# A graph layer's edge sums: 72 directly summed columns instead of 48, with three bf16 addends in place of fp32 operands

## The chip, the cores and the metric

The kernel runs on one NeuronCore of a Trainium2 chip. The metric is the device time of one execution in microseconds (us), lower is better. All times, spans and durations below come from that core.

## The reference

`x` has 6250 nodes with 128 features, there are 206250 edges, each with 128 fp32 features, and `src` names the node of each edge. What is computed, cut to what matters:

```python
edge_aggr = zeros((6250, 128)).at[src].add(edge_attr)            # sum of each node's edges
combined  = concatenate([x, edge_aggr, global_expand], -1) @ W_c + b_c
h = softplus(combined @ W1 + b1)
h = softplus(h @ W2 + b2)
x = layernorm(x + h @ W3 + b3)
```

Nearly all of the time goes into the first line: the edges are in no order of `src`, so each of the 206250 rows has to find its node.

## The kernel before

**Columns and groups.** The edges are laid out as 128 partitions by 1612 columns (the last is partial); a column is 128 edges. Columns 0 to 47 are summed directly. The other 1564 go through ten groups (`GROUPS`: 40, 120, 200, 240, 240, 240, 212, 140, 88 and 44 columns, called groups 0 to 9 here). For a group, DVE and PE work out a position for each edge (`positions`), so that edges of the same block of 256 nodes stand together in DRAM. POOL then writes each column to its positions with one indirect DMA (`scatter_rows`, L644). When the whole group is written, it is read back in chunks of 1024 rows (`reduce_steps`): DVE makes a one-hot matrix `hot` of 8 tiles of 128 rows against 256 nodes (L423), PE multiplies (L437: 8 tiles of 128x256, each recorded as two fp32 matmuls, so "x16"), and DVE adds the product onto `sums_t` (L454). While group g is scattered, group g-1 is reduced.

**The direct sum.** `direct_steps` takes columns in sets of 12 (`SET`). For each set and each of 13 windows of 512 nodes, ACT makes a one-hot of two columns: two `Abs` of 128x512 (L577) and one `Relu` of 128x1024 (L579), into `direct_hot`, of which there are four buffers. PE multiplies the columns' rows with it (L589: two fp32 matmuls of 512, recorded as four), adding up in the PSUM tile `direct_sum` (two buffers). After the set's 12 columns DVE adds that tile onto `sums_t` (L593). Two columns in one window are one *job* here: 24 x 13 = 312 jobs. The multiplication of a job stands two jobs behind its comparison.

**The order of the work.** PE, DVE, ACT and SP follow an order written out by hand: whatever stands first in an engine's queue holds up what is behind it. The main loop goes through *pieces* of 10 columns. For piece i it issues, in this order: the loading of the rows of piece i+3 (SP's queue), a copy of the node codes next to the rows of piece i+2 (ACT, L636), the ten scatters of piece i (POOL), and then a share of everything else: the next group's positions, the reduction of the group before, in groups 3 to 5 also the transposes and products of the nodes' own features, and a share of the direct steps. A scatter needs its piece's copy L636, and that copy stands in ACT's queue behind all direct comparisons of the steps before it.

The direct steps are spread over groups 1 to 6 in proportion to `left`:

```python
left[g] = max(0.0, groups[g][1] - groups[g][0]
              - groups[g - 1][3] * groups[g - 1][2] / 3 - (9 if 3 <= g < 6 else 0))
...
direct_at += len(direct) * left[g] / sum(left) / len(mine)
```

that is: the group's columns, less a third of the tiles of the reduction that runs in it, less 9 where the nodes' work is placed. There are 64, 168, 296, 336, 336, 336, 308, 188, 136 and 68 tiles in groups 0 to 9. So groups 1 to 6 have shares of 98.7, 144.0, 132.3, 119.0, 119.0 and 100.0.

After group 9's reduction, three small layers and the layer norm finish the nodes.

Of the kernel before, what the change touches and what calls it, by code (L numbers as in the profile page):

```python
# [7 lines left out]
F32 = mybir.dt.float32  # L8
BF16 = mybir.dt.bfloat16
# [3 lines left out]
ALU = mybir.AluOpType  # L13
# [3 lines left out]
P = 128  # L17
# [2 lines left out]
LOAD_COLS = 10  # L20
EPS = 1e-5

GROUPS = ((40, 1), (120, 2), (200, 4), (240, 4), (240, 4), (240, 4), (212, 4), (140, 2), (88, 2),
          (44, 1))
CHUNK_ROWS = 1024
PLACES = 3

DIRECT = 48
SET = 12
WIDE = 512  # L30
QUAD = 2
FILL = 4
POS_COLS = 20
PART_COLS = 60
# [13 lines left out]
def kernel(  # L48
# [23 lines left out]
    nc = tc.nc  # L72
    N, D = x.shape
# [8 lines left out]

    ND = min(DIRECT, T) // QUAD * QUAD
    c0 = ND
# [83 lines left out]
    with ExitStack() as phase:  # L168
        keep = phase.enter_context(tc.tile_pool(name="keep", bufs=1))
# [4 lines left out]
        direct_p = phase.enter_context(tc.tile_pool(name="direct", bufs=1))  # L174
# [17 lines left out]
        def whole_nodes(c0, c1):  # L192
            n = c1 - c0
            part = src_i[:, c0:c1]
            node = per.tile([P, C_MAX], F32, name="node", bufs=1)[:, :n]
            wrap = per.tile([P, C_MAX], F32, name="wrap", bufs=1)[:, :n]
            nc.vector.tensor_copy(node, part)
            nc.vector.tensor_scalar(wrap, node, 0.0, float(N), op0=ALU.is_lt, op1=ALU.mult)
            nc.vector.tensor_add(node, node, wrap)
            nc.vector.tensor_scalar(node, node, -1.0, float(N), op0=ALU.max, op1=ALU.min)  # L200
            nc.vector.tensor_scalar(wrap, node, 0.0, float(N + 1), op0=ALU.is_lt, op1=ALU.mult)
            nc.vector.tensor_add(part, node, wrap)
            return part, node, wrap
# [341 lines left out]
        def direct_steps():  # L545


            steps = []
            if not ND:
                return steps  # L550
            NW = -(-NB * BL // WIDE)
            less = keep.tile([P, NW, ND], F32, name="less")
            rows_in, hot_of, sum_of = {}, {}, {}

            def begin():

                first = keep.tile([P, NW], F32, name="first")
                nc.gpsimd.iota(first, pattern=[[WIDE, NW]], base=0, channel_multiplier=0,
                               allow_small_or_imprecise_dtypes=True)
                part, node, _ = whole_nodes(0, ND)  # L560
                nc.vector.tensor_copy(node, part)
                nc.vector.tensor_tensor(
                    less, node.unsqueeze(1).to_broadcast([P, NW, ND]),
                    first.unsqueeze(2).to_broadcast([P, NW, ND]), op=ALU.subtract)

            def load(c):
                n = min(SET, ND - c)
                rows_in[c] = direct_p.tile([P, SET, D], F32, name="direct_rows", bufs=2)
                sync_dma(rows_in[c][:, :n],
                         edge_attr[:P * T, :].rearrange("(p t) d -> p t d", p=P)[:, c:c + n, :])  # L570

            def compare(c, w, q):
                n = min(WIDE, NB * BL - w * WIDE)
                hot = direct_p.tile([P, QUAD, WIDE], F32, name="direct_hot", bufs=4)
                hot_of[c, w, q] = hot
                for j in range(QUAD):
                    nc.scalar.activation(hot[:, j, :n], iota_f[:, :n], AF.Abs,  # L577
                                         bias=less[:, w, c + q + j:c + q + j + 1], scale=-1.0)
                nc.scalar.activation(hot[:, :, :n], hot[:, :, :n], AF.Relu, bias=ones[:, :1],  # L579
                                     scale=-1.0)  # L580

            def add(c, w, q):
                n = min(WIDE, NB * BL - w * WIDE)
                k = min(SET, ND - c)
                hot = hot_of.pop((c, w, q))
                if q == 0:
                    sum_of[c, w] = ps.tile([P, WIDE], F32, name="direct_sum", bufs=2)
                for j in range(QUAD):
                    nc.tensor.matmul(sum_of[c, w][:, :n], rows_in[c][:, q + j, :], hot[:, j, :n],  # L589
                                     start=(q + j == 0), stop=(q + j == k - 1))  # L590
                if q + QUAD == k:
                    here = sums_t[:, w * WIDE:w * WIDE + n]
                    nc.vector.tensor_add(here, here, sum_of.pop((c, w))[:, :n])  # L593

            jobs = [(c, w, q) for c in range(0, ND, SET) for w in range(NW)
                    for q in range(0, min(SET, ND - c), QUAD)]
            steps += [begin, lambda: load(0)]
            for i in range(len(jobs) + 2):
                def one(i=i):
                    if i < len(jobs):  # L600
                        c, w, q = jobs[i]
                        if (w, q) == (NW // 2, 0) and c + SET < ND:
                            load(c + SET)
                        compare(*jobs[i])
                    if i > 1:
                        add(*jobs[i - 2])
                steps.append(one)
            return steps
# [10 lines left out]
        def load_rows(i):  # L619
            if i >= len(pieces):  # L620
                return
            g, c, k, r = pieces[i]
            rows = rows_p.tile([P, LOAD_COLS, W], F32, name="rows")
            rows_at[i] = rows
            if r == P:
                rows_dma(
                    rows[:, :k, :D],
                    edge_attr[:P * T, :].rearrange("(p t) d -> p t d", p=P)[:, c:c + k, :])
            else:
                rows_dma(rows[:r, 0, :D], edge_attr[P * T:, :])  # L630
# [21 lines left out]
        with tc.manual_schedule(engines={ET.PE, ET.DVE, ET.Activation, ET.SP}):  # L652
            nc.scalar.add_instruction(mybir.InstLoadActFuncSet(
                name=nc.get_next_instruction_name(), act_func_set_id=TABLES))
# [32 lines left out]
            direct = direct_steps()  # L687
# [3 lines left out]
            for g in range(1, G - 3):  # L691
                left[g] = max(0.0, groups[g][1] - groups[g][0]
                              - groups[g - 1][3] * groups[g - 1][2] / 3 - (9 if 3 <= g < 6 else 0))
            direct_at = 0.0
            i = 0
            assert G > 6
            nodes = []
            for g in range(G):
                mine = [q for q in range(len(pieces)) if pieces[q][0] == g]
                prep = []  # L700
                if g + 1 < G:
                    prep = [lambda g=g: node_codes(*groups[g + 1][:2])] + positions(g + 1)
                sums = reduce_steps(g - 1) if g else []

                if g == 3:
                    nodes = node_rows()
                other = nodes[:-(-len(nodes) // (6 - g))] if 3 <= g < 6 else []
                if 3 <= g < 6:
                    nodes = nodes[len(other):]
                filled = fill_rows(g + 1)  # L710
                done = [0, 0, 0, 0]
                for q in mine:
                    load_rows(i + LEAD)
                    code_rows(i + LEAD - 1)
                    scatter_rows(i)
                    i += 1

                    now = []
                    for w, todo in enumerate((prep, sums, other, filled)):
                        share = (q - mine[0] + 1) / len(mine)  # L720
                        if w == 2:
                            share = (share - 0.8) / 0.15
                        else:
                            share = share / AHEAD[w]
                        share = max(0.0, min(1.0, share))
                        upto = int(round(len(todo) * share))
                        now.append(todo[done[w]:upto])
                        done[w] = upto
                    if left[g]:
                        k = int(direct_at + 0.5)  # L730
                        direct_at += len(direct) * left[g] / sum(left) / len(mine)
                        now.append(direct[k:int(direct_at + 0.5)])

                    for _, _, step in sorted(
                            (((k + 0.5) / len(part), w, step) for w, part in enumerate(now)
                             for k, step in enumerate(part)), key=lambda t: t[:2]):
                        step()
# [111 lines left out]
    with tc.manual_schedule(engines={ET.PE, ET.DVE, ET.Activation, ET.SP}):  # L849
# [3 lines left out]
        for step in range(len(order) + 2):  # L853

            first, second, third = (order[k] if 0 <= k < len(order) else None
                                    for k in (step, step - 1, step - 2))
# [9 lines left out]
            if third:  # L866
                k = part_of[third]
# [29 lines left out]
```

## Time and profile before

| what | value |
|---|---|
| median of three runs | 2163.2 us (2162.69 to 2173.22) |
| the profiled execution's own time | 2166.67 us |
| its span, first to last instruction | 2164.9 us |
| mean granted TensorE clock | 0.925 |
| PE busy | 1789.7 us (83%) |
| POOL busy | 1560.2 us (72%) |
| DVE busy | 1328.0 us (61%) |
| ACT busy | 912.7 us (42%) |
| POOL, indirect DMAs (L644), 1564 of them | 1503.2 us |
| PE, reduction (L437) | 1106.0 us |
| PE, direct sum (L589) | 559.0 us |
| DVE, one-hots of the reduction (L423) | 592.2 us |
| ACT, direct comparisons (L577, L579) | 404.6 and 348.0 us |

A group's line on the profile's page names the source line, the engine, the operation and the tiles (out<-in), then the count, the busy time, the mean duration of one in ns, and behind the second bar the idle time of the engine just before such instructions and what ended most of it. In the timeline a line has its start and its length in us, and in brackets the idle time of the engine before it and what released it. The scatters run from 25.6 to 2019.3 us.

### The profile page before, as it was taken

What the parts mean: (1) busy time and instruction counts of PE and PEld (TensorE: products, weight loads), DVE (VectorE), ACT (ScalarE), POOL (GpSimd) and SP (SyncE); (2) the same over time, 40 slices, a digit from 0 to 9 for tenths busy, and PEclk for the clock granted to TensorE, in tenths of its full rate; (3) what the DMA queues carried; (4) which work ended last, traced back from release to release, by engine and by line L of the source; (5) the groups of instructions that cost most, each with busy time, mean ns of one, the idle gap of its engine ahead of it and who ended that gap; (6) DMA issues with size and microseconds to landing.
All of it is one profiled execution on the core that took longest, in us unless ns stands there. A gap on an engine that the chain in (4) does not pass through costs nothing.

```text
span 2164.9 us, 22230 instructions
## 1 busy us (share of the span) xinstructions
PE 1789.7 (83%) x6415; PEld 1209.0 (56%) x6415; DVE 1328.0 (61%) x1923; ACT 912.7 (42%) x1350; POOL 1560.2 (72%) x1631
## 2 busy tenths in 40 slices
PE   3398788966889878999889998788998899688884
PEld 0144445534555555666556666556666778566752
DVE  7386457524656345675465855355755798796567
ACT  0476665653444335444353443353342000006964
POOL 5777777777777767777777777777777777777226
PEclk8699999987999999999999999999999999899997
DMA  9998788738786665676756666556766687776521
GB/s 299 303 313 270 216 256 251 231 101 262 213 225 189 194 193 148 188 207 188 198 173 180 194 190 175 169 167 189 202 198 170 211 245 227 214 213 199 151 75 60
DMA packets 415376, 435.50 MB, mean 201 GB/s; under 512 B 37743, under 2 KB 305766, under 8 KB 415254
## 3 DMA queue, kind: packets, MB, share of 16 engines
q1 hardware_dynamic: 365062, 330.71, 54.9%
q0 software_dynamic: 50048, 103.35, 14.4%
q8 instruction: 51, 0.84, 0.2%
q14 instruction: 71, 0.58, 0.1%
q10 hardware_dynamic: 144, 0.02, 0.0%
HBM read 260.90 MB, written 173.03 MB: 200 GB/s over the span
## 4 chain that ended last, share of the span: by engine, by line
PE 57%; DVE 15%; POOL 9%; issue 7%; DMA 6%; ACT 4%; DVEq 1%; SPq 0%; POOLq 0%; ACTq 0%
PE part L437 37%; PE direct_sum L589 16%; POOL place L644 8%; DVE hot L423 7%; DMA place<-rows,pos 4%; DVE sums_t L454 2%; ACT hot L418 2%; DVE so_far L316 1%; DVE sums_t L593 1%; DMA rows<-in_edge_attr 1%; DMA chunks<-place 1%; PE small L339 1%; POOL y L833 1%; DVEq L448 1%; DVE pos L350 1%
## 5 line engine op out<-in xcount | busy, mean ns | idle before, releaser
L644 POOL DMA_INDIRECT place<-rows,pos x1564 | 1503.2, 961 | 509.0 <-issue 443.5
L437 PE MATMUL part<-hot,chunks 128*128 128x256 f32 x4472 | 1106.0, 405 | 267.8 <-DVE hot L423 250.9
L437 PEld LDWEIGHTS part<-hot,chunks 128*128 128x128 f32 x4472 | 894.9, 203 | 507.8 <-DVE hot L423 310.5
L577 ACT ACTIVATE direct_hot<-iota_f,less 128x512 f32<-128x512 f32 (+1 forms) x624 | 404.6, 695 | 811.0 <-PE direct_sum L589 808.1
L423 DVE SCALAR_TENSOR_TENSOR hot<-chunks,iota_ps 128x2048 f32<-128x2048 f32 (+1 forms) x261 | 592.2, 2270 | 44.2 <-DMA chunks<-place 44.2
L589 PE MATMUL direct_sum<-direct_hot,direct_rows 128*128 128x512 f32 (+1 forms) x1248 | 559.0, 580 | 29.4 <-DMA direct_rows<-in_edge_attr 25.6
L454 DVE TENSOR_TENSOR sums_t<-sums_t,part 128x256 f32 x781 | 327.1, 419 | 133.3 <-PE part L437 110.8
L589 PEld LDWEIGHTS direct_sum<-direct_hot,direct_rows 128*128 128x128 f32 x1248 | 233.3, 190 | 232.2 <-issue 204.9
L579 ACT ACTIVATE direct_hot<-direct_hot,ones 128x1024 f32<-128x1024 f32 (+1 forms) x312 | 348.0, 1115 | 10.1
L593 DVE TENSOR_TENSOR sums_t<-sums_t,direct_sum 128x512 f32<-128x512 f32 (+1 forms) x52 | 34.7, 667 | 410.5 <-PE direct_sum L589 410.5
L636 ACT COPY rows<-src_i 128x10 f32<-128x10 f32 (+1 forms) x159 | 30.7, 196 | 360.3 <-DMA place<-rows,pos 328.9
L350 DVE TENSOR_REDUCE pos<-at 128x20 int32<-128x500 f32 (+2 forms) x80 | 87.0, 1087 | 2.7
L316 DVE TENSOR_TENSOR_SCAN so_far<-iota_ps,ib 128x1500 bf16<-128x1500 f32 (+5 forms) x29 | 85.7, 2955 | 0.0
L418 ACT ACTIVATE hot<-iota_f,chunks 128x256 f32<-128x256 f32 x156 | 64.2, 493 | 26.7 <-DMA chunks<-place 24.2
L845 POOL TENSOR_TENSOR x_sb<-x_sb,b_all 128x512 f32<-128x512 f32 (+1 forms) x13 | 15.2, 1219 | 67.8 <-DMA x_sb<-in_x 67.8
L348 DVE TENSOR_TENSOR at<-small,ib 128x500 f32<-128x500 f32 (+2 forms) x80 | 52.9, 661 | 4.2 <-PE small L339 3.5
L833 POOL TENSOR_SCALAR y<-y,mv,rs 128x128 f32<-128x128 f32 (+1 forms) x45 | 35.2, 796 | 19.9 <-DVE rs L827 19.0
L262 DVE TENSOR_TENSOR ib<-block,iota_ps 128x1500 bf16<-128x1500 bf16 (+5 forms) x29 | 44.2, 1550 | 0.0
L273 PE MATMUL small<-ib,ones_h 128*128 128x500 bf16 (+2 forms) x80 | 23.8, 406 | 23.9 <-DVE ib L262 23.9
L536 DVE TENSOR_SCALAR z_x<-small,z_bias 128x512 f32<-128x512 f32 (+1 forms) x13 | 9.3, 718 | 51.3 <-PE small L534 51.3
L335 PE MATMUL small<-so_far,ones_h 128*128 128x500 bf16 (+2 forms) x80 | 31.4, 393 | 11.1 <-DVE last L319 11.1
L420 ACT ACTIVATE hot<-hot,ones 128x2048 f32<-128x2048 f32 (+1 forms) x20 | 39.2, 1960 | 0.7
(115 smaller groups left out, 472.7 us busy)
## 6 DMA issues: line engine op xcount, KB each, us to landing
chunks<-place SPq DMA_DIRECT2D x278, 516.0 KB, 4.5
rows<-in_edge_attr SPq DMA_DIRECT2D x155, 640.0 KB, 6.7
place<-fill SPq DMA_DIRECT2D x252, 258.0 KB, 8.3
place<-rows,pos POOLq DMA_INDIRECT x1564, 4.5
x_sb<-in_x SPq DMA_DIRECT2D x24, 256.0 KB, 4.6
direct_rows<-in_edge_attr SPq DMA_DIRECT2D x4, 768.0 KB
out<-y SPq DMA_DIRECT2D x12, 256.0 KB, 2.2
chunks<-place SPq DMA_DIRECT2D x3, 258.0 KB, 3.2
```

Of the source, the lines that this page charges most:

```text
L316: nc.vector.tensor_tensor_scan(t, iota_ps[:, 1:2].to_broadcast([P, NB * n]), in_block[k][0], 0.0, op0=ALU.mult, op1=ALU.add)
L350: nc.vector.tensor_reduce(pos[:, a - c0 + j0:a - c0 + j1], at.rearrange("p b g -> p g b"), axis=mybir.AxisListType.X, op=ALU.add)
L418: nc.scalar.activation(hot[:, j], codes, AF.Abs, bias=chunks[i][:, j, D:W], scale=-1.0)
L423: nc.vector.scalar_tensor_tensor(hot[:, :m], chunks[i][:, :m, D:W].to_broadcast([P, m, BL]), code_of(g), iota_ps.unsqueeze(1).to_broadcast ...
L437: nc.tensor.matmul(part[:, s - q, :], t[:, s * sub + j, :D], hot[:, s * sub + j], start=(j == 0), stop=(j == sub - 1))
L454: nc.vector.tensor_add(here, here, part[:, s - q, :])
L577: nc.scalar.activation(hot[:, j, :n], iota_f[:, :n], AF.Abs, bias=less[:, w, c + q + j:c + q + j + 1], scale=-1.0)
L579: nc.scalar.activation(hot[:, :, :n], hot[:, :, :n], AF.Relu, bias=ones[:, :1], scale=-1.0)
L589: nc.tensor.matmul(sum_of[c, w][:, :n], rows_in[c][:, q + j, :], hot[:, j, :n], start=(q + j == 0), stop=(q + j == k - 1))
L593: nc.vector.tensor_add(here, here, sum_of.pop((c, w))[:, :n])
L644: s = nc.gpsimd.indirect_dma_start(out=dst, out_offset=bass.IndirectOffsetOnAxis(ap=at, axis=0), in_=rows[:r, j, :], in_offset=None)
L833: engine.tensor_scalar(y[:r, q, :], y[:r, q, :], mv[:r, at + q, 0:1], rs[:r, 1, at + q:at + q + 1], op0=ALU.subtract, op1=ALU.mult)
```

## The change

`DIRECT` goes from 48 to 72, and group 6 from 212 to 188 columns, so that 24 columns are summed directly instead of being scattered and reduced. The fp32 operands of the direct matmuls become bf16. Each fp32 number x is written as three bf16 numbers whose sum is x: the upper half of its bits, the upper half of what is then left, and the rest. DVE does this in `split`, two columns at a time with three instructions; the first two addends are put into the two halves of the fp32 row itself, the third into a new tile `direct_low`. The one-hots, which hold ones and zeros, become bf16 tiles. A job now has six bf16 matmuls instead of two fp32 ones. There are 36 x 13 = 468 jobs, and 6 sets x 13 = 78 additions of `direct_sum` instead of 52. The window offsets `less` are computed for each set instead of once. The load of the first set moves ahead, to group 0's last piece. Group 6's reduction has 284 tiles instead of 308. The core of the diff:

```diff
-GROUPS = ((40, 1), (120, 2), (200, 4), (240, 4), (240, 4), (240, 4), (212, 4), (140, 2), (88, 2),
+GROUPS = ((40, 1), (120, 2), (200, 4), (240, 4), (240, 4), (240, 4), (188, 4), (140, 2), (88, 2),
...
-DIRECT = 48
+DIRECT = 72
...
+SPLIT = 2
...
+            def halves(t):
+
+                return [t.bitcast(BF16).rearrange("p c (d h) -> p c d h", h=2)[:, :, :, h]
+                        for h in (0, 1)]
+
+            def split(c):
+
+                n = min(SET, ND - c)
+                less = less_of[c] = direct_p.tile([P, NW, SET], F32, name="less", bufs=2)
+                nc.vector.tensor_tensor(
+                    less[:, :, :n], node_f[:, c:c + n].unsqueeze(1).to_broadcast([P, NW, n]),
+                    first.unsqueeze(2).to_broadcast([P, NW, n]), op=ALU.subtract)
+                low_in[c] = direct_p.tile([P, SET, D], BF16, name="direct_low", bufs=2)
+                for a in range(0, min(SET, ND - c), SPLIT):
+                    b = min(a + SPLIT, SET, ND - c)
+                    rest = direct_p.tile([P, SPLIT, D], F32, name="direct_rest")[:, :b - a]
+                    x_c = rows_in[c][:, a:b]
+                    nc.vector.tensor_sub(rest, x_c, halves(x_c)[1])
+                    nc.vector.tensor_sub(low_in[c][:, a:b], rest, halves(rest)[1])
+
+                    nc.vector.tensor_copy(halves(x_c)[0], halves(rest)[1])
...
-                hot = direct_p.tile([P, QUAD, WIDE], F32, name="direct_hot", bufs=4)
+                hot = direct_p.tile([P, QUAD, WIDE], BF16, name="direct_hot", bufs=4)
...
-                for j in range(QUAD):
-                    nc.tensor.matmul(sum_of[c, w][:, :n], rows_in[c][:, q + j, :], hot[:, j, :n],
-                                     start=(q + j == 0), stop=(q + j == k - 1))
+                for j in range(q, q + QUAD):
+                    addends = halves(rows_in[c][:, j:j + 1]) + [low_in[c][:, j:j + 1]]
+                    for i, part in enumerate(addends):
+                        nc.tensor.matmul(sum_of[c, w][:, :n], part[:, 0], hot[:, j - q, :n],
+                                         start=(j == 0 and i == 0), stop=(j == k - 1 and i == 2))
...
-            steps += [begin, lambda: load(0)]
+
+            steps += [lambda: load(0), begin, lambda: split(0)]
...
+                        if (w, q) == (NW - 2, 0) and c + SET < ND:
+                            split(c + SET)
...
+            direct_first = direct[:1]
+            direct = direct[1:]
...
+                    if g == 0 and q == mine[-1]:
+                        for step in direct_first:
+                            step()
```

More of the change, by code (lines that the diff above doesn't have):

```diff
@@ L551, in direct_steps @@
             NW = -(-NB * BL // WIDE)
-            less = keep.tile([P, NW, ND], F32, name="less")
-            rows_in, hot_of, sum_of = {}, {}, {}
+            node_f = keep.tile([P, ND], F32, name="node_f")
+            first = keep.tile([P, NW], F32, name="first")
+            less_of = {}
+            rows_in, low_in, hot_of, sum_of = {}, {}, {}, {}
             def begin():
-                first = keep.tile([P, NW], F32, name="first")
                 nc.gpsimd.iota(first, pattern=[[WIDE, NW]], base=0, channel_multiplier=0,
                                allow_small_or_imprecise_dtypes=True)
[L560 to L564, printed above, removed]
+                part, _, _ = whole_nodes(0, ND)
+                nc.vector.tensor_copy(node_f, part)
             def load(c):
@@ L577, in compare @@
                     nc.scalar.activation(hot[:, j, :n], iota_f[:, :n], AF.Abs,
-                                         bias=less[:, w, c + q + j:c + q + j + 1], scale=-1.0)
+                                         bias=less_of[c][:, w, q + j:q + j + 1], scale=-1.0)
                 nc.scalar.activation(hot[:, :, :n], hot[:, :, :n], AF.Relu, bias=ones[:, :1],
```

## Prediction

> **What bounds the kernel now.** I read first the page's groups, then POOL's waits, the timeline at the longest of them, and last a table of stages. The page:
>
> ```profile
> L644 POOL DMA_INDIRECT place<-rows,pos x1564 | 1503.2, 961 | 509.0 <-issue 443.5
> ```
>
> A scatter takes 0.96 us, and 0.30 pass before the next: 1.265 us a column, 12.65 a piece of ten. 1564 x 1.265 = 1978 of the 1994 us between the first scatter and the last; nearly nothing holds POOL up. Taken alone this says that 24 columns fewer save 24 x 1.265 = **30.4 us**. But a second chain runs level with POOL. POOL's longest wait behind the copy L636 is 9.3 us:
>
> ```profile
> 811.05 0.19 ACT L636 COPY rows<-src_i 128x10 f32<-128x10 f32 x1
> ...
> 811.52 0.96 POOL L644 DMA_INDIRECT place<-rows,pos  x1 [9.28 <-ACT rows L636]
> ```
>
> The copy came late, because it stands in ACT's queue behind direct comparisons, which wait for PE to free `direct_hot`. So I compared, over the run, when the copy for the third piece of a group was made (ACT's first work in that group) and when that piece was scattered: group 3 465.3 and 511.6, group 4 816.0 and 824.2, group 5 1123.5 and 1127.9, group 6 1432.2 and 1432.7 (POOL waits 1.46 us), group 7 1686.2 and 1700.9. In groups 1 and 2 the lead is above 36 us, as far as the row buffers allow; group 3 eats it up, and from there to group 6 ACT's copies come just in time. The stages between these copies (us; PE, PEld, DVE, ACT and POOL busy; clock; DMA share; GB/s):
>
> ```profile
> 465.00:816.00 351.00, 274.61 (x921) 181.96 (x921) 167.20 (x196) 140.02 (x200) 259.79 (x271) 0.87 0.71 205
> 816.00:1123.50 307.50, 273.32 (x976) 183.58 (x975) 188.33 (x227) 132.66 (x184) 233.48 (x244) 0.96 0.66 190
> 1123.50:1432.20 308.70, 270.08 (x968) 184.75 (x967) 180.41 (x216) 127.64 (x185) 233.69 (x244) 0.95 0.63 179
> 1432.20:1686.20 254.00, 229.10 (x864) 163.26 (x863) 155.49 (x176) 100.86 (x150) 192.62 (x201) 0.97 0.64 183
> ```
>
> PE is busy for 87 to 90% of the last three. The rest is the wait for one-hots, 96.0 us in 42 pieces from 816 to 1686. One of them:
>
> ```profile
> 913.35 1.88 PE L589 MATMUL direct_sum<-direct_hot,direct_rows 128*128 128x512 f32 x4
> ...
> 915.07 0.38 PE L334 MATMUL small<-ib,upto_h 128*128 128x500 bf16 x1
> ...
> 915.26 0.69 DVE L593 TENSOR_TENSOR sums_t<-sums_t,direct_sum 128x512 f32<-128x512 f32 x1 [9.07 <-PE direct_sum L589]
> ...
> 915.28 0.37 PE L335 MATMUL small<-so_far,ones_h 128*128 128x500 bf16 x1
> ...
> 915.49 0.37 PE L336 MATMUL small<-more,ones_h 128*128 128x500 bf16 x1
> ...
> 915.87 2.28 DVE L423 SCALAR_TENSOR_TENSOR hot<-chunks,iota_ps 128x2048 f32<-128x2048 f32 x1
> ...
> 918.21 4.97 PE L437 MATMUL part<-hot,chunks 128*128 128x256 f32 x14 [2.03 <-DVE hot L423]
> ```
>
> DVE waits 9 us in its queue for the job that ends a window, adds it (L593), and only then makes the next one-hot; PE stands idle for it. PE, with these waits, is the bound of groups 3 to 6 beside POOL. So the question is whether the change makes that chain longer.
>
> **The change part by part.**
>
> *Scatters.* 24 fewer, -30.4 us, only where POOL paces. From group 7 on, after the last direct step, it does: the rest then follows the scatters, so the end moves as group 7's third piece does.
>
> *A job on PE.* Before, four records: 913.35 to 915.07, 1.72 us. After, six bf16 matmuls of 512. The nearest rows are L334 to L336 above: starts 0.21 apart with 500 columns, weight loads hidden; six make 1.29. Three quarters of the cost, one and a half times the jobs. The addends' loads read every second bf16; bf16 loads took 0.10 and fp32 ones 0.19, both hidden in the rows, and 0.19 would still fit under 0.21, so I cost them at nothing.
>
> On that price the Trainium skill disagrees with itself: "TensorE: Matmul & The Clock Gate", section "Back-to-back issue gap", gives about 131 ns for a sustained 512-column matmul with its load, and 216 isolated. By 131 a job would be 0.79, and POOL would pace to the end. The 0.21 of the rows here is against it.
>
> *Jobs per group.* The direct steps go from 316 to 472 (the load left out), and the shares of `left` fall only in group 6, to 76.0, of 689 in sum. Groups 1 to 6 get 67.6, 98.6, 90.7, 81.5, 81.5, 52.1 steps after, against 43.7, 63.8, 58.6, 52.7, 52.7, 44.3. PE's change: group 3 90.7 x 1.29 - 58.6 x 1.72 = +16.2; groups 4 and 5 105.1 - 90.6 = +14.5 each; group 6 67.2 - 76.2 = -9.0. The reductions in groups 3 to 6 stay: the 24 tiles saved are group 6's, multiplied in group 7, where PE isn't the bound.
>
> *A job on ACT.* Each comparison is queued ahead of the copies:
>
> ```profile
> 462.89 1.32 ACT L577 ACTIVATE direct_hot<-iota_f,less 128x512 f32<-128x512 f32 x2
> 464.24 1.15 ACT L579 ACTIVATE direct_hot<-direct_hot,ones 128x1024 f32<-128x1024 f32 x1
> 465.29 0.19 ACT L636 COPY rows<-src_i 128x10 f32<-128x10 f32 x1
> ```
>
> 2.475 us. No row shows ACT writing bf16 one-hots; bounds: half of it and, by the mean durations (711 and 1148), 2.57; I take 2.475, the row of the same shapes. In group 1 there are 5.6 jobs a piece: 14.1 us with the copy, above POOL's 12.65; in group 2 4.9 jobs, 12.4. Before it was 9.2 and 8.1. So ACT becomes the bound of groups 1 and 2. It starts at 60.6 as before; 164 jobs and 34 copies make 406 + 7: group 3's first copy at 474 at the earliest, against 465.3, and with waits for PE, of which ACT had 107 in that stretch before, later. I take +10: 484 (bounds 465, where bf16 is cheaper, and 515). POOL's deadline, 511.6, still holds there.
>
> The skill's "ScalarE: Activation LUTs", section "What ACT_TABLE_LOAD costs", says that an ACTIVATE costs the same per element in fp32 and bf16; no run here shows that yet, and it speaks against a gain on ACT.
>
> *More additions L593.* In groups 3 to 6 there are 51 (15, 13, 14, 9) instead of 35 (10, 8, 9, 8). Each holds up DVE's queue, the next one-hot behind it, and PE. Mean wait: 96.0 / 42 = 2.3 us; the longer ones in group 3 took 4.7. 16 x 2.3 = +37 (bounds: +75, and -45, if the denser jobs cover 1.3 us at each of the old 35).
>
> *Split.* Per set 18 DVE instructions on 256 elements; the nearest row, L199 with 240, took 0.41: 7.6 us a set, with the next one-hot, and PE, queued behind. Three fall into groups 3 to 5; of each, PE's lead covers a part: 3 x 3 = +9 (bounds 0 and 23). The first, in group 1, and its earlier load ahead of one row load in SP's queue cost nothing: POOL has a lead above 36 us there; without it 2 to 3 us.
>
> *The sum.* The chain needs 465.3 to 816.0 for group 3, less one boundary wait of 24.1 (PE ahead of the chunks, which it won't be): 326.6; then 307.5, 308.7, 254.0. With PE's changes 342.8, 322.0, 323.2, 245.0 = 1233; with additions and splits 1279. From 484 that gives 1763 for the copy that group 7's third piece waits for. Before, that piece was scattered at 1700.9: +62, against -30 and more if POOL paced. The profiled execution's 2166.7 becomes about 2229; its median runs lie 3.5 lower: **2225 us**, 2.9% slower.
>
> **Rivals.** *POOL keeps pace* (faster): 2163.2 - 30.4 = 2133. For it: PE idles over 10% of these stages. Against: each wait is DVE's order, not a lack of work. It needs a chain 100 us shorter, a job of 0.95 us or less. *Only the multiplications count* (within 0.5%): no more waits at additions, and ACT at its floor: 474 + 1233 = 1707, +6: 2169. *ACT's pace spoils more than groups 1 and 2*: 515 + 1233 + 75 + 23 = 1846, +145: 2308. It decides from the point where the copies of group 2 come later than their scatters.
>
> **How the numbers follow.** This kernel's measurement tells about 0.5% from no change, 2152 to 2174. Forecast 0.66; POOL keeps pace 0.13; only the multiplications 0.09; ACT spoils more 0.12. So faster 0.13, same 0.09, slower 0.78. The range: down past the floor for cheaper additions, up towards the third rival, 2146 to 2295.
>
> **What would show it.** In the profile after: scatters still 0.96 us with 0.30 between, but POOL's wait for L636 tens of us instead of 12.3, at the ends of groups 3 to 6; a job's six matmuls in about 1.3 us; ACT near 100% busy in groups 1 and 2; 78 additions with PE idle behind many. I am wrong if POOL doesn't wait for L636, or if a bf16 job takes under 1 us.

## The result, and the profile after

The changed kernel takes **2274.15 us** (median of four runs, 2273.88 to 2275.02) against 2163.52: a ratio of 1.0501, with a 95% interval from 1.0471 to 1.0531. The forecast was 2225, the range 2146 to 2295. The profiled execution took 2274.32 us (span 2272.5, mean granted clock 0.947); its forecast was 2229. The first four experiments ran in one series at the usual pace (before: 2166.97 there), the second to the fourth with one execution each; in the eight later runs every kernel, the one before included, took some 30% longer (the "long pace" below), so each of those is read by its ratio to the kernel before in the same series.

The page's groups after the change. A line is followed by the count, the busy time, the mean duration of one, and the idle time ahead of such instructions with its main releaser:

```profile
L673 POOL DMA_INDIRECT place<-rows,pos x1540 | 1479.4, 961 | 641.6 <-issue 425.1
L439 PE MATMUL part<-hot,chunks 128*128 128x256 f32 x4424 | 1092.7, 405 | 269.6 <-DVE hot L425 253.1
...
L601 ACT ACTIVATE direct_hot<-iota_f,less 128x512 bf16<-128x512 f32 (+1 forms) x936 | 605.2, 693 | 617.2 <-PE direct_sum L615 614.3
L615 PE MATMUL direct_sum<-direct_hot,direct_rows 128*128 128x512 bf16 (+1 forms) x1872 | 540.0, 372 | 83.5 <-ACT direct_hot L603 50.2
...
L619 DVE TENSOR_TENSOR sums_t<-sums_t,direct_sum 128x512 f32<-128x512 f32 (+1 forms) x78 | 52.0, 667 | 548.4 <-PE direct_sum L615 548.4
```

A scatter still takes 0.961 us and POOL still passes 0.30 us of issue after each, yet its idle time rose from 509.0 to 641.6 us. The waits of the kernel after say where from (total, times, longest):

```profile
POOL place L673 <- ACT rows L665: 157.1, 41, 11.4
```

In the kernel before:

```profile
POOL place L644 <- ACT rows L636: 12.3, 7, 9.3
```

POOL no longer paces groups 3 to 6; it waits for ACT's copies of the node codes, and these stand behind comparisons that wait for PE. The stages between the copies for the third pieces of groups 3 to 7, after (us; PE, PEld, DVE, ACT and POOL busy; clock; DMA share; GB/s):

```profile
518.50:869.40 350.90, 289.17 (x1239) 186.86 (x1239) 184.39 (x237) 217.04 (x299) 231.53 (x242) 0.94 0.65 184
869.40:1216.30 346.90, 294.87 (x1249) 197.55 (x1249) 192.67 (x239) 193.75 (x269) 230.19 (x240) 0.93 0.60 168
1216.30:1547.90 331.60, 285.08 (x1240) 191.87 (x1240) 187.00 (x238) 196.20 (x271) 229.17 (x239) 0.95 0.59 168
1547.90:1800.90 253.00, 224.50 (x985) 162.11 (x985) 155.53 (x176) 119.72 (x170) 177.59 (x186) 0.96 0.65 179
```

Together 1282.4 us, where the kernel before took 1221.2. PE was busy for 1093.6 of them (before 1047.1). The third piece of group 7 was scattered at 1810.2 instead of 1700.9: +109.3. The end came 107.7 later, so nothing of weight happens behind it.

One place of the timeline after shows a job and an addition (start and length in us, then what was done; in brackets the idle time ahead and its releaser):

```profile
949.80 0.59 PE L615 MATMUL direct_sum<-direct_hot,direct_rows 128*128 128x512 bf16 x2
...
950.24 0.38 PE L615 MATMUL direct_sum<-direct_hot,direct_low 128*128 128x512 bf16 x1
...
950.45 0.59 PE L615 MATMUL direct_sum<-direct_hot,direct_rows 128*128 128x512 bf16 x2
...
950.88 0.38 PE L615 MATMUL direct_sum<-direct_hot,direct_low 128*128 128x512 bf16 x1
...
951.10 0.59 PE L615 MATMUL direct_sum<-direct_hot,direct_rows 128*128 128x512 bf16 x2
...
952.60 0.69 DVE L619 TENSOR_TENSOR sums_t<-sums_t,direct_sum 128x512 f32<-128x512 f32 x1 [9.87 <-PE direct_sum L615]
...
953.20 3.27 DVE L318 TENSOR_TENSOR_SCAN so_far<-iota_ps,ib 128x1500 bf16<-128x1500 f32 x1
...
957.03 2.28 DVE L425 SCALAR_TENSOR_TENSOR hot<-chunks,iota_ps 128x2048 f32<-128x2048 f32 x1
...
959.36 4.87 PE L439 MATMUL part<-hot,chunks 128*128 128x256 f32 x11 [6.80 <-DVE hot L425]
```

The next job begins at 951.10, 1.30 us behind the one of 949.80: six matmuls, 0.217 apart. DVE waited 9.87 us for the window's last job, added the window's sum, and had a scan of 3.27 us to do before the next one-hot; PE stood idle for 6.80.

### The profile page after: what moved, and what is told of

Its sections match the earlier page's. It is cut to its first block, busy times and chain, and to the rows that moved or that the text cites. A ratio compares the mean times of both kernels' runs of the same rounds, so it can differ in the third digit from the quotient of the medians.

```text
span 2272.5 us, 25751 instructions
## 1 busy us (share of the span) xinstructions
PE 1847.1 (81%) x7922; PEld 1236.1 (54%) x7922; DVE 1369.5 (60%) x2051; ACT 1267.9 (56%) x1815; POOL 1536.2 (68%) x1607
## 4 chain that ended last, share of the span: by engine, by line
PE 56%; DVE 17%; DMA 8%; ACT 7%; issue 6%; POOL 5%; DVEq 1%; SPq 0%; ACTq 0%; POOLq 0%
PE part L439 36%; PE direct_sum L615 16%; DVE hot L425 8%; POOL place L673 5%; DMA place<-rows,pos 4%; DMA place<-fill 2%; ACT direct_hot L601 2%; DVE sums_t L456 2%; DVE so_far L318 2%; ACT hot L420 2%; ACT direct_hot L603 1%; DVE sums_t L619 1%; DVEq L450 1%; PE small L341 1%; DVE at L350 0%
## 5 line engine op out<-in xcount | busy, mean ns | idle before, releaser
L673 POOL DMA_INDIRECT place<-rows,pos x1540 | 1479.4, 961 | 641.6 <-issue 425.1
L601 ACT ACTIVATE direct_hot<-iota_f,less 128x512 bf16<-128x512 f32 (+1 forms) x936 | 605.2, 693 | 617.2 <-PE direct_sum L615 614.3
L615 PE MATMUL direct_sum<-direct_hot,direct_rows 128*128 128x512 bf16 (+1 forms) x1872 | 540.0, 372 | 83.5 <-ACT direct_hot L603 50.2
L425 DVE SCALAR_TENSOR_TENSOR hot<-chunks,iota_ps 128x2048 f32<-128x2048 f32 x258 | 585.3, 2270 | 13.5 <-DMA chunks<-place 13.5
L603 ACT ACTIVATE direct_hot<-direct_hot,ones 128x1024 bf16<-128x1024 bf16 (+1 forms) x468 | 521.9, 1115 | 15.2
L619 DVE TENSOR_TENSOR sums_t<-sums_t,direct_sum 128x512 f32<-128x512 f32 (+1 forms) x78 | 52.0, 667 | 548.4 <-PE direct_sum L615 548.4
L615 PE MATMUL direct_sum<-direct_hot,direct_low 128*128 128x512 bf16 (+1 forms) x936 | 347.7, 372 | 0.0
L615 PEld LDWEIGHTS <-direct_rows 128*128 128x128 bf16 x1872 | 181.2, 98 | 287.8 <-issue 80.8
L665 ACT COPY rows<-src_i 128x10 f32<-128x10 f32 (+1 forms) x156 | 29.9, 194 | 304.2 <-DMA place<-rows,pos 280.2
L615 PEld LDWEIGHTS <-direct_low 128*128 128x128 bf16 x936 | 91.6, 98 | 103.3 <-issue 1.0
L352 DVE TENSOR_REDUCE pos<-at 128x20 int32<-128x500 f32 (+1 forms) x79 | 85.5, 1083 | 2.7
L350 DVE TENSOR_TENSOR at<-small,ib 128x500 f32<-128x500 f32 (+1 forms) x79 | 52.0, 658 | 4.3 <-PE small L341 3.8
L867 POOL TENSOR_SCALAR y<-y,mv,rs 128x128 f32<-128x128 f32 (+1 forms) x45 | 35.1, 800 | 19.8 <-DVE rs L861 18.6
L337 PE MATMUL small<-so_far,ones_h 128*128 128x500 bf16 (+1 forms) x79 | 31.0, 393 | 10.6 <-DVE last L321 10.6
```

The lines of the kernel that those rows point to most:

```text
L350: nc.vector.tensor_mul(at, got.pop((k, j0)), in_block[k][1][:, :, j0:j1])
L352: nc.vector.tensor_reduce(pos[:, a - c0 + j0:a - c0 + j1], at.rearrange("p b g -> p g b"), axis=mybir.AxisListType.X, op=ALU.add)
L425: nc.vector.scalar_tensor_tensor(hot[:, :m], chunks[i][:, :m, D:W].to_broadcast([P, m, BL]), code_of(g), iota_ps.unsqueeze(1).to_broadcast ...
L601: nc.scalar.activation(hot[:, j, :n], iota_f[:, :n], AF.Abs, bias=less_of[c][:, w, q + j:q + j + 1], scale=-1.0)
L615: nc.tensor.matmul(sum_of[c, w][:, :n], part[:, 0], hot[:, j - q, :n], start=(j == 0 and i == 0), stop=(j == k - 1 and i == 2))
L673: s = nc.gpsimd.indirect_dma_start(out=dst, out_offset=bass.IndirectOffsetOnAxis(ap=at, axis=0), in_=rows[:r, j, :], in_offset=None)
```

## The experiments

The theory on trial is the prediction's: the chain through PE, with its waits for DVE and its exchange with ACT, sets the time of groups 3 to 6, and 24 more columns make it longer. The rivals: POOL's pace, ACT alone, the splits, the price of a bf16 product.

**1. bf16 with 48 columns.** The change without the new number of columns.

```diff
-GROUPS = (..., (188, 4), ...)
-DIRECT = 72
+GROUPS = (..., (212, 4), ...)
+DIRECT = 48
```

> The bf16 addends alone: 48 columns and the groups of before. Chain theory (PE's work and its waits for one-hots bound groups 3 to 6): 208 jobs there cost 0.43 us less each, about 90 us off a chain of 1221, so POOL paces everywhere, its waits for the copies of node codes nearly vanish, and the time is 2150 to 2160, just below before's 2163. Rival, the split on DVE and what it holds up are the cost: slower than before, 2175 or more. Rival, ACT is the bound: no difference from before, since ACT does the same number of comparisons, 2160 to 2166.

Measured: 2156.49 us (2155.4 to 2160.38), ratio 0.9958, interval 0.9944 to 0.9972. It beats both kernels, as the chain theory expected (2150 to 2160); with 48 columns the splits, which were to make it 2175 or more if they were the cost, cost nothing that shows. The third pieces' copies of groups 4 to 7 now come 22 to 39 us ahead of their scatters, and of POOL's waits for L665 0.6 us are left. Those waits were 12.3 us in the kernel before: 2167.0 - 12.3 = 2154.7. So bf16 takes PE off the path, and what the time gains by it is about all that POOL had been waiting. The 24 further columns cost 2274.15 - 2156.49 = **118 us** (the kernel before differed by 3 us between these two series).

**2. 72 columns in fp32.** No split, fp32 rows and one-hots, one matmul for each column and window.

```diff
-                    addends = halves(rows_in[c][:, j:j + 1]) + [low_in[c][:, j:j + 1]]
-                    for i, part in enumerate(addends):
-                        nc.tensor.matmul(sum_of[c, w][:, :n], part[:, 0], hot[:, j - q, :n],
-                                         start=(j == 0 and i == 0), stop=(j == k - 1 and i == 2))
+                    nc.tensor.matmul(sum_of[c, w][:, :n], rows_in[c][:, j, :], hot[:, j - q, :n],
+                                     start=(j == 0), stop=(j == k - 1))
```

> 72 columns alone: fp32 rows and fp32 one-hots, no split, all else as after the change. Chain theory: 306 jobs in groups 3 to 6 cost 0.43 more each than in bf16, +131 us, and some of the 166 in groups 1 and 2: 2400 to 2450. Rival, ACT is the bound: same as after the change, 2260 to 2290, since ACT's work is the same. Rival, the split is the cost: faster than after the change, below 2260.

Measured: 2393.99 us, just below the expectation. The same columns cost 227 us over the kernel before in fp32, and 111 in bf16, each against its own series. The stages after group 3's third copy take 1370.1 us instead of 1282.4, +87.7; that copy itself comes 33.3 us later. By the price of a job, 306 of them at 1.72 instead of 1.29 us should have made +131, less 9 for the splits. PE is busy for 1216.4 of the 1370.1 us, 122.8 more, and idle for 153.7, 35.1 less; so over a quarter of the higher price is hidden in time in which PE waited anyway.

**3. One addend of three.** PE multiplies only the third addend; the two others, and so most of each number, are left out. Comparisons, splits and additions stay.

```diff
-                    addends = halves(rows_in[c][:, j:j + 1]) + [low_in[c][:, j:j + 1]]
+                    addends = [low_in[c][:, j:j + 1]]
```

> After the change, but only the third addend of each number is multiplied: two of three matmuls are left out, so the direct sums are not the reference's. ACT, DVE and POOL do what they did. Chain theory: a job costs PE 0.43 instead of 1.29, 260 us less in groups 3 to 6, so POOL paces there and what is left is ACT's lag in groups 1 and 2: 2133 to 2165. Rival, ACT is the bound: 2250 to 2275. Rival, the split and the additions on DVE: 2220 to 2275.

Measured: 2123.34 us, 10 below the range of the chain theory, which had left out the old waits, and far from both rivals. That is POOL's pace: the 24 scatters (30.4) and the old waits (12.3) make 2167.0 - 42.7 = 2124.3. The page of this kernel:

```profile
L673 POOL DMA_INDIRECT place<-rows,pos x1540 | 1477.8, 960 | 493.8 <-issue 440.0
```

POOL's idle time is below that of the kernel before. All comparisons on ACT, all splits and all 78 additions are in here, and they don't hold POOL up as long as PE has little to multiply. The 151 us up to 2274 come with the products.

**4. No Relu.** The second step of the comparison is left out, and the distances themselves are multiplied; a job takes ACT 1.33 instead of 2.475 us.

```diff
-                nc.scalar.activation(hot[:, :, :n], hot[:, :, :n], AF.Relu, bias=ones[:, :1],
-                                     scale=-1.0)
```

> After the change without the Relu of each comparison: the one-hots are not ones and zeros, and the sums are not the reference's. A job costs ACT 1.33 us instead of 2.48, PE and DVE do the same. Chain theory: only what ACT spoils in groups 1 and 2 comes back, 25 to 40 us: 2230 to 2250; groups 3 to 6 stay, with POOL waiting over 100 us for the copies. Rival, ACT is the bound to the end of group 6: POOL paces, 2135 to 2165.

Measured: 2225.99 us, 48 less than the changed kernel and 4 below the range of the chain theory. The copy for group 3's third piece comes at 488.9 instead of 518.5 (-29.6), and the stages up to group 7 take 1263.3 instead of 1282.4 (-19), where the theory had expected nothing. In these stages PE's waits for `direct_hot` (20.9 us in the kernel after) are gone. ACT does have a part, above all in groups 1 and 2. What PE, DVE, ACT and POOL did there from 105 to 224 us, first in the kernel after:

```profile
105.00:224.00 119.00, 101.10 (x432) 53.90 (x431) 79.38 (x127) 109.84 (x146) 90.27 (x95) 0.97 1.00 285
```

with one addend:

```profile
105.00:224.00 119.00, 85.42 (x265) 46.37 (x269) 79.43 (x122) 117.13 (x156) 90.25 (x95) 0.74 0.99 280
```

and without Relu:

```profile
105.00:224.00 119.00, 106.82 (x455) 57.47 (x463) 82.40 (x133) 63.72 (x106) 90.37 (x95) 0.97 0.98 282
```

The columns after the length are PE, PEld, DVE, ACT and POOL. With little to multiply ACT is busy for 98% of the stretch, without Relu PE for 90%, and in the kernel after neither reaches its own limit: 92 and 85%. Group 3's third copy came at 484.6 with one addend (near ACT's limit), at 488.9 without Relu (near PE's), and at 518.5 with both in full. With the other relieved, each engine was done by 489; with both loaded they needed 30 us more.

**5. No splits.** DVE's splits are left out, and the upper half is multiplied three times, so the two smaller addends are missing from the sum.

```diff
-                    nc.vector.tensor_sub(rest, x_c, halves(x_c)[1])
-                    nc.vector.tensor_sub(low_in[c][:, a:b], rest, halves(rest)[1])
-
-                    nc.vector.tensor_copy(halves(x_c)[0], halves(rest)[1])
...
-                    addends = halves(rows_in[c][:, j:j + 1]) + [low_in[c][:, j:j + 1]]
+                    addends = halves(rows_in[c][:, j:j + 1])[1:] * 3
```

> After the change without the splits: the upper half of each row is multiplied three times, so the sums are not the reference's; PE has the same six matmuls a job, ACT and POOL the same work, DVE 41.7 us less and one link less before the first job. If the prediction's term for the splits holds (3 us for each of those in groups 3 to 5, little before): 5 to 20 us less than 2274, 2254 to 2269. Rival, the splits and what they hold up are a main cost: under 2235.

Measured: 3007.83 us beside 2826.49 for the kernel before; ratio 1.0575, interval 1.0477 to 1.0673. At this pace the 5 to 20 us of the expectation can't be told from nothing; the run is read with the next and the last experiment.

**6. Late additions.** Each addition L619 is issued four jobs later, so that DVE finds its product done; everything else is as in the changed kernel.

```diff
+LATE = 4
...
-                    here = sums_t[:, w * WIDE:w * WIDE + n]
-                    nc.vector.tensor_add(here, here, sum_of.pop((c, w))[:, :n])
+                    def put_sum():
+                        here = sums_t[:, w * WIDE:w * WIDE + n]
+                        nc.vector.tensor_add(here, here, sum_of.pop((c, w))[:, :n])
+                    late.append((jobs.index((c, w, q)) + 2 + LATE, put_sum))
...
+                    while late and late[0][0] <= i:
+                        late.pop(0)[1]()
```

> After the change, but DVE adds a finished window onto the sums four jobs later than it could, so that it need not stand waiting for PE's last job of the window with the next one-hot behind it. PE, ACT and DVE do the same work. If the wait at these additions is what the prediction says (51 of them in groups 3 to 6, 2.3 us and more each, with the slower clock after a gap up to 7): 60 to 150 us less, 2125 to 2215. Rival, PE's work alone is the bound and the waits would only move: 2255 to 2275.

Measured: 2878.8 us beside 2826.49, on the same chip as experiment 5; ratio 1.0146, interval 1.0095 to 1.0196. It beats the kernel without splits by 129 us, although it does all of the splits. Two further series gave 1.0139 and 1.014:

> The late additions with 72 columns once more, since the transfers of the last series were slow for every kernel, the kernel before too. If the wait at the additions is what the prediction says: 60 to 150 us less than 2274, 2125 to 2215. Rival, PE's work alone is the bound and the waits would only move: 2255 to 2275.

Measured: 2903.56 beside 2862.84 us, ratio 1.0139, interval 1.0101 to 1.0177.

> The late additions with 72 columns a third time, for a series in which the kernel before takes its 2163. If the wait at the additions is what the prediction says: 60 to 150 us less than 2274, 2125 to 2215. Rival, PE's work alone is the bound and the waits would only move: 2255 to 2275. The trace should show nearly no wait of DVE for a finished window, and PE's waits for one-hots in groups 3 to 6, 166 us after the change, down to a third.

Measured: 2882.0 beside 2840.73 us, ratio 1.014, interval 1.009 to 1.019. That was again at the long pace, so what late additions are worth at the usual one wasn't measured.

**7. Late additions, and the first set's load ahead of group 0.**

```diff
-            direct_first = direct[:1]
+            direct[0]()
...
-                    if g == 0 and q == mine[-1]:
-                        for step in direct_first:
-                            step()
```

> As the late additions, and the first set of direct rows is loaded before group 0's pieces instead of at the end of group 0, where its transfer landed only at 85.6 us with DVE waiting 25.4 us for it. Theory: the chain starts 15 to 25 us sooner and, where the chain is still the bound, the end comes that much sooner than with the late additions alone; where POOL paces already, only its wait of 9.2 us for the first set goes. Rival, the load only pushes others back in the same queue: no difference from late additions.

Measured: 2876.59 us, ratio 1.0131, interval 1.0026 to 1.0236, on the same chip as experiment 6. The earlier load can't be told from none.

**8. The same with 60 columns** (`DIRECT = 60`, group 6 with 200 columns), in two series.

> Late additions, early first load, and 60 columns instead of 72 (group 6 has 200): 12 more scatters than with 72, +15 us where POOL paces, and a sixth fewer direct jobs. Theory: POOL paces nearly throughout, 2135 to 2148: faster than before, than the bf16 addends alone and, if the 72-column version is still held by ACT or PE, than that one.

> Late additions, first set loaded early, 60 columns, once more. Theory: POOL paces nearly throughout, 2135 to 2148, that is 2163 less 15 for 12 scatters less up to 10 for the waits for copies that go. Rival, ACT or PE still holds it up in the first groups: 2150 to 2180.

Measured: 2867.65 beside 2826.49 us, ratio 1.0114 (1.0017 to 1.0211), and 2906.81 beside 2862.84, ratio 1.0147 (1.0111 to 1.0183). Both series had been expected to beat the kernel before; at this pace they don't. With late additions, 60 and 72 columns can't be told apart here.

**9. The changed kernel once more**, at the long pace.

> The changed kernel as it is, for a ratio of its own beside those of the runs with late additions (1.014 each time) and without splits (1.0575). If this chip holds the instructions back as in the last three series: were the waits of VectorE for each column's last product what the late additions saved, the ratio lies at 1.05 to 1.06, with the waits of TensorE for one-hots near 440 us, as without splits; were the late additions worth nothing, and the splits what makes the difference, it lies under 1.03. If the chip runs as in the first series: about 2274, a ratio of 1.05.

Measured: 3044.7 beside 2868.51 us; ratio 1.0668, interval 1.0571 to 1.0765. Its five executions spread from 2999.37 to 3048.47 us, so the loss at this pace is better put at 5 to 7%. Late additions take it to 1.4%, with an interval that lies far below; the 5.75% without the splits can't be told from it. DVE's additions and PE's waits for DVE's one-hots, the kernel after at the long pace:

```profile
L619 DVE TENSOR_TENSOR sums_t<-sums_t,direct_sum 128x512 f32<-128x512 f32 (+1 forms) x78 | 52.0, 667 | 964.1 <-remote 511.5
...
PE part L439 <- DVE hot L425: 436.6, 70, 43.0
```

with late additions (experiment 6):

```profile
L621 DVE TENSOR_TENSOR sums_t<-sums_t,direct_sum 128x512 f32<-128x512 f32 (+1 forms) x78 | 51.8, 665 | 181.5 <-remote 123.9
...
PE part L440 <- DVE hot L426: 158.2, 35, 63.6
```

and PE's waits without splits (experiment 5):

```profile
PE part L439 <- DVE hot L425: 437.5, 70, 42.0
```

Only the move of the additions takes most of PE's wait away. The stages from group 3's third copy to group 7's took 1719.8, 1543.2 and 1729.3 us in these three. But over half of the 964.1 us is no wait of the kind that the prediction priced. "remote" stands for a signal whose sender the profile doesn't show. One such place in experiment 9:

```profile
1313.89 0.38 PE L615 MATMUL direct_sum<-direct_hot,direct_low 128*128 128x512 bf16 x1
...
1324.18 0.69 DVE L619 TENSOR_TENSOR sums_t<-sums_t,direct_sum 128x512 f32<-128x512 f32 x1 [20.39 <-remote]
```

By the profile the last product before it ended at 1314.27, 9.9 us before the addition began (the ends of matmuls are modelled there, so whether the product or its signal was late isn't shown). At the usual pace the page above has all 548.4 us of that wait ended by PE's product. So at the long pace moving the additions is shown to save most of the loss, in part perhaps by avoiding delays that the usual pace doesn't have. What the additions cost at the usual pace stays open.

## Why the forecast was right in sign and 49 us short

**POOL's pace: right.** "24 fewer, -30.4 us, only where POOL paces" held in experiment 3 to about a microsecond, once the 12.3 us are added that POOL waited before. The rival "POOL keeps pace" gave 2133 and left those out; its condition, "a job of 0.95 us or less", was met there by leaving out two addends and not by the change.

**The signs.** POOL's waits for the copies (157.1 us), the job of 1.30 us and PE idle behind additions all came. "ACT near 100% busy in groups 1 and 2" did not: it was busy for 92, 84 and 90% from 105 to 224, to 380 and to 520 us.

**A job on PE: right.** 1.29 forecast, 1.30 in the timeline. The Trainium skill's "TensorE: Matmul & The Clock Gate", section "Back-to-back issue gap", gives about 131 ns for a matmul of 512 columns in a sustained stream with weight loads, and 216 for an isolated one. This stream had a weight load for each matmul, hidden, and ran 0.217 apart: the measurement decides for the larger figure. Reading every second bf16 cost nothing, as assumed: a weight load of the interleaved halves took 98 ns, and so did one of the dense third addend.

**A job on ACT: right.** Shape by shape, the comparisons take 710 and 1148 ns with bf16 output, 711 and 1148 before. The skill's "ScalarE: Activation LUTs", section "What ACT_TABLE_LOAD costs", says that fp32 and bf16 cost the same per element; this trace agrees.

**The chain of groups 3 to 6: right in sum, partly by luck.** 1279 forecast, 1282.4 measured. PE's busy time grew by 46.5 us (forecast 36.2 for the jobs). Its idle time was 1221.2 - 1047.1 = 174.1 before, less the boundary wait of 24.1 that did go, 150.0; after, 1282.4 - 1093.6 = 188.8. That is +38.8, where I had 46 for additions and splits together. About half of it, 20.9, is PE's waits for ACT's one-hots, which I had not priced; its waits for DVE's grew only from 146 to 166. In the kernel after:

```profile
PE part L439 <- DVE hot L425: 165.7, 66, 6.8
PE direct_sum L615 <- ACT direct_hot L603: 20.9, 22, 1.1
```

in the kernel before, with the boundary wait of 24.1:

```profile
PE part L437 <- DVE hot L423: 170.3, 57, 24.1
```

So additions and splits cost PE less than half of what I had put, and the 10 us more of busy time and the 20.9 that I had left out filled the difference: the sum is within 3.4 us by luck. The single groups missed by 5 to 10 us, in both directions. The splits' 9 us stay untested at this size.

**The step that was mis-sized: "I take +10: 484".** Group 3's third copy came at 518.5, 34.5 later, beyond even the bound of 515. The 164 jobs ahead of it were as forecast, and ACT began at 60.3. But I worked out ACT's floor and added ten microseconds for its waits; they were 68.5, in 19 pieces:

```profile
ACT direct_hot L601 <- PE direct_sum L615: 68.5, 19, 19.5
```

The miss would have been 58 us, had the floor not been too high: ACT's own work up to there was 389.7 us (518.5 - 60.3 - 68.5) instead of 413. Jobs follow each other after 2.42 us in the trace, not 2.475, and 12 of the 164 fell on the last window, which is half as wide. One of the 19 pieces is the load that I had put at nothing:

```profile
58.27 16.59 SPq L147 DMA_DIRECT2D place<-fill  x14
...
75.92 0.33 SPq L147 DMA_DIRECT2D direct_rows<-in_edge_attr  x1
...
85.63 0.48 DVE L591 TENSOR_TENSOR direct_rest<-direct_rows 128x256 f32<-128x256 f32 x1 [25.35 <-DMA direct_rows<-in_edge_attr]
...
86.84 1.04 PE L615 MATMUL direct_sum<-direct_hot,direct_rows 128*128 128x512 bf16 x2 [32.19 <-DVE direct_rows L594]
...
89.62 1.33 ACT L601 ACTIVATE direct_hot<-iota_f,less 128x512 bf16<-128x512 f32 x2 [19.49 <-PE direct_sum L615]
```

This is the timeline of the kernel after. The change moves the load ahead in the code, but SP's queue was busy with 14 fills until 74.9 us, and the rows came only then. DVE waited for them in its first split, PE for the split, ACT for PE. The kernel before had a like wait in ACT (17.85 us, up to 93.05), which the sum leaves out. With the earlier load it stayed. How much of the 34.5 it makes wasn't told apart: at the long pace the earlier load of experiment 7 gained nothing.

The rest, 49 us in 18 pieces, is the step that I left out. I priced PE from group 3 on, and ACT alone before it. In experiment 4, with ACT relieved, groups 1 and 2 took PE until 489, and in experiment 3, with PE relieved, they took ACT until 485; with both loaded they take until 518.5. At piece 27, in group 2 at 379 us, the copy's lead was down to 0.5 us. That is about the point from which my third rival, "ACT's pace spoils more", was to decide, and its first term, 515, is what happened. Its other bounds, 75 and 23 for additions and splits, did not, so the time lies between the forecast and that rival.

**The end: 9.3 us short.** I took group 7's third scatter to follow its copy at once. The pieces before it were late as well, and POOL then needs 12.65 us for each, so it came 9.3 later. In all 34.5 + 3.4 + 9.3 = 47.2 us make the 1763 of the forecast the 1810.2 of the trace. The stretch behind it took 1.6 us less than before, and the 3.5 us that I took off for the median were only 0.2 this time; that makes the 49.

## What to carry to other kernels

Work that is taken from one bound engine and given to two others must be priced on both of these at once: two engines that passed four buffers between them, both near their limit, finished 30 us later than the slower one did with the other relieved. An in-order queue that waits for its newest result holds up what a third engine needs next: at the long pace, issuing the additions four jobs later took most of the loss away, and at the usual pace that is still to be measured. A cheaper operation is worth what the path shows: bf16 alone gained 10.5 us, about what POOL had waited, and spending it on half as many columns again cost 118.

## What was not expected of the hardware

At the long pace no instruction is much longer (a matmul of the reduction takes 417 ns on average in experiment 6, 405 in the kernel after), but they come late. PE in experiment 6, in a stretch in which it waited for nothing that the profile shows:

```profile
1302.68 0.38 PE L440 MATMUL part<-hot,chunks 128*128 128x256 f32 x1 [0.93 <-issue]
1304.07 0.38 PE L440 MATMUL part<-hot,chunks 128*128 128x256 f32 x1 [1.01 <-issue]
1305.47 1.49 PE L440 MATMUL part<-hot,chunks 128*128 128x256 f32 x2 [1.03 <-issue]
```

Elsewhere in the same trace 16 such matmuls run in 3.62 us. PE waited 421 us in all for "issue" in that kernel (239.7 and 181.3 in its two main lines), and the DMA queues moved 150 GB/s instead of 190, while a one-hot on DVE took 2.270 us and a scatter 0.962, as ever. The cause isn't settled. The granted clock was 0.81 to 0.85 in all these runs, and 0.90 to 0.95 in those at the usual pace but one; that one, experiment 3, had 0.854, so the clock alone isn't shown to make the difference. Nor is it the chip alone: the same one, number 11, ran experiments 1 to 4 and experiment 9.
